# Dense experts of two blocks side by side, and two sparse batches beside two dense ones

## The chip, the cores and the metric

The kernel runs on one core of one Trainium2 chip. The metric is the time of one execution on the device in microseconds, as the median of several runs. The core has five engines that each follow an instruction queue of their own, in order: TensorE (matmuls and transposes; PE in the profile, with PEld for its weight loads), VectorE (DVE), ScalarE (ACT), GpSimd (POOL) and SyncE (SP), which here only starts DMA transfers. An instruction that has to wait for another engine holds up everything behind it in its own queue.

## The reference

The input x has 4 batches of 1024 tokens with 128 numbers each. Four layers follow, each added to x after a layer norm: causal softmax attention (16 heads of 64), an expert layer, linear attention with running sums, and the expert layer again with the same weights. The change concerns the expert layer:

```
logits = einsum('bsh,eh->bse', x, router_w)            # 32 experts
rw = softmax(logits)
vals, idx = top_k(rw, 2)
w_masked = zeros_like(rw) with vals at idx
out = sum over e of (x * w_masked[:, e]) @ W_e          # W_e is 128 x 128
```

Only two weights per token differ from zero, so the same sum can be formed in two ways: with all 32 experts for every token ("dense"), or with two experts for each token after the tokens were sorted by expert ("sparse").

## The kernel before

Tokens are kept in `x_sb` as 32 blocks of 128; a batch is eight blocks, and four blocks are a quarter.

**Dense.** `dense` (L923) takes a list of quarters. For each block it goes through 8 groups `g` of 4 experts: one matmul (recorded as two) into a PSUM tile `pe` of 512 columns (L949), and then the weighting. For the groups in `ACT_GROUPS` (1, 4 and 6) ScalarE scales the four parts into a tile `t` (L957), GpSimd adds the tiles of a block up (L963) and folds the sum in half twice (L977, L978). For the other five groups VectorE does four `scalar_tensor_tensor` each (L966): a part of `pe` times the token's weight, added to `xs`, the block's 128 columns of `x_sb`. All 20 of a block go to the same `xs`, one after the other. `settle` (L931) adds GpSimd's sum two blocks later and stores four finished blocks if wanted. After each group `beside(turn)` is called, so a quarter has 32 turns; also one step of `routed` (L846), which prepares router weights `w` and the transposed tokens of the next quarter.

**Sparse.** `experts` (L197) is a generator for one batch, a chain of steps that end with `yield`. It finds each token's two experts (L209 to L267), counts them with prefix sums on GpSimd and two matmuls (L273 to L290), works out a row for each token and expert (L295 to L333), scales the tokens into tiles `xw` with 8 buffers (L367) and puts closures into `queue` that scatter them to DRAM in 16 indirect DMAs (L357). Each scatter is followed by a small memset (L361). Then comes the pass (L389): 47 tiles of 128 sorted rows in 12 groups of up to four, with 15 iterations. An iteration loads one group of rows (L393), the weights of the group before (L398; for the 15 overflow tiles L402 reads the number of the expert into a register and L405 loads one weight), transposes one group (L424) and multiplies another (L413), which is stored (L419). The flag `passing[0]` lets one chain at a time into the pass. Last, 16 indirect fetches (L432) bring the results back, VectorE adds them (L459, L464), and the batch is stored (L465).

**Order.** The scheduling is manual: each engine's queue has the order in which the Python code emits instructions. After attention there are three stages:

- "f": dense for the two quarters of batch 3, with `fill` (L1094) beside it. It advances two `prepare` generators for linear attention, and takes an entry of `queue` every fourth turn (the fetches of batch 2).
- the linear stage: 32 units, whose first operand is `products(0)` (L1121). In its last units `routed` prepares the first quarter of the next stage.
- "s": dense for six quarters (batches 1 to 3) beside one sparse chain (batch 0). `pieces` (L1237) takes an entry of `queue` every second turn, and calls `on` (L1081) at 5 of 8 turns, or 3 of 8 during the pass. `on` advances each chain by one step if `queue` has at most four entries. What is left after the last turn follows in a plain loop (L1250).

Of the kernel before, what the change touches and what calls it, by code (L numbers as in the profile page):

```python
# [20 lines left out]
def hybrid_kernel(  # L21
# [175 lines left out]
    def experts(b, nm, banks, queue, room, came=None):  # L197
# [80 lines left out]
        yield  # L278

# [102 lines left out]
        while passing[0]:  # L382
            yield
        passing[0] = True
# [4 lines left out]
        for i in range(len(groups) + 3):  # L389
# [19 lines left out]
            if 0 <= i - 3:  # L409
# [9 lines left out]
                nc.sync.dma_start(out=yv[:, g : g + n, :], in_=ys[:, :n, :])  # L419
            if 0 <= i - 2 < len(groups):  # L420
                g, n = groups[i - 2]
                pt = banks[0].tile([P, 512], F32, tag="ps1", name=f"pxs_{nm}_{g}")
                for c in range(n):
                    nc.tensor.transpose(pt[:, c * P : (c + 1) * P], xs[g][:, c, :], ident)  # L424
                xsT[g] = xo.tile([P, 512], F32, tag="xsT", bufs=2, name=f"xsT_{nm}_{g}")
                s_.copy(xsT[g][:, : n * P], pt[:, : n * P])
# [406 lines left out]
    xp = ctx.enter_context(tc.tile_pool(name="xp", bufs=1, reuse_waits="tile"))  # L833
    came = ctx.enter_context(tc.tile_pool(name="came", bufs=3, reuse_waits="tile"))
# [88 lines left out]
    def dense(nm_, qs, store, pool, mp, ps_e, known, beside):  # L923


        due = []
# [12 lines left out]
        for i, q in enumerate(qs):  # L939
# [4 lines left out]
            for c in range(4):  # L944
                xs = x_sb[:, q * 4 + c, :]
                parts = []
                for g in range(E // 4):
                    pe = ps_e.tile([P, 512], F32, tag="e", name=f"pe_{nm_}_{q}_{c}_{g}")
                    nc.tensor.matmul(  # L949
                        pe, xnT[:, c * P : (c + 1) * P],  # L950
                        we_sb[:, 4 * g : 4 * g + 4, :].rearrange("p e d -> p (e d)"),
                        start=True, stop=True,
                    )
                    if g in ACT_GROUPS:
                        t = mp.tile([P, 512], F32, tag="t", name=f"t_{nm_}_{q}_{c}_{g}")
                        for e in range(4):
                            nc.scalar.mul(  # L957
                                t[:, e * D : (e + 1) * D], pe[:, e * D : (e + 1) * D],
                                w[:, c, 4 * g + e : 4 * g + e + 1],
                            )  # L960
                        parts.append(t)
                        if len(parts) > 1:
                            nc.gpsimd.tensor_tensor(parts[0], parts[0], t, ALU.add)  # L963
                    else:
                        for e in range(4):
                            nc.vector.scalar_tensor_tensor(  # L966
                                xs, pe[:, e * D : (e + 1) * D],
                                w[:, c, 4 * g + e : 4 * g + e + 1], xs,
                                ALU.mult, ALU.add,
                            )  # L970
                    if g == 3:
                        settle(2)
                    next(nxt, None)
                    beside(turn)
                    turn += 1
                s = parts[0]
                nc.gpsimd.tensor_tensor(s[:, :256], s[:, :256], s[:, 256:], ALU.add)  # L977
                nc.gpsimd.tensor_tensor(s[:, :D], s[:, :D], s[:, D : 2 * D], ALU.add)  # L978
                due.append((xs, s, q * 4 if c == 3 else None))
# [11 lines left out]
    lb = lin.enter_context(tc.tile_pool(name="lb", bufs=3, reuse_waits="tile"))  # L991
    G = 4
# [87 lines left out]

    def on():  # L1081
# [5 lines left out]
    with ExitStack() as ph:  # L1087
        mp = ph.enter_context(tc.tile_pool(name="mpf", bufs=9, reuse_waits="tile"))
# [5 lines left out]
        def fill(turn):  # L1094

            next(preps[turn % 2], None)
# [17 lines left out]
    with lin as ph:  # L1114
        lp = ph.enter_context(tc.tile_pool(name="lp", bufs=3, reuse_waits="tile"))
# [4 lines left out]

        def products(u):  # L1121

            kq, va = feats[u // G]
            k = kq[:, u % G, :P]
            kv = lp.tile([P, NE, LH, LD], F32, tag="kv", bufs=3, name=f"kv_{u}")
            nc.gpsimd.tensor_tensor(
                kv[:, :LD],
                k.rearrange("p (h d) -> p h d", h=LH).unsqueeze(1).to_broadcast([P, LD, LH, LD]),
                va[:, u % G, :].rearrange("p (h e) -> p e h", e=LD).unsqueeze(3).to_broadcast([P, LD, LH, LD]),
                ALU.mult,  # L1130
            )
            nc.scalar.copy(kv[:, LD].rearrange("p h d -> p (h d)"), k)
            return kv
# [73 lines left out]
        qs = list(range(NB // 4 * 1, NT // 4))  # L1207
        kv = products(0)
# [25 lines left out]
    for b, r in enumerate((room,)):  # L1234
        sides.append(experts(b, f"s{b}", banks, queue, r, came))

    def pieces(turn):  # L1237

        if turn % 2 and queue:
            queue.pop(0)()  # L1240
        if turn % 8 in ((0, 3, 6) if passing[0] else (0, 2, 3, 5, 6)):
            on()

    with ExitStack() as ph:
        mp = ph.enter_context(tc.tile_pool(name="mps", bufs=12, reuse_waits="tile"))
        ps_s = ph.enter_context(tc.tile_pool(name="ps_2", bufs=3, space=PSUM, reuse_waits="tile"))
        ps_e = ph.enter_context(tc.tile_pool(name="ps_es", bufs=5, space=PSUM, reuse_waits="tile"))
# [38 lines left out]
```

## Time and profile before

| | us |
|---|---|
| median of three runs | 2052.43 (2049.49 to 2055.55) |
| the profiled execution | 2047.43 |
| its span, first to last instruction | 2045.7 |
| stage f, first to last dense matmul | 1497.5 to 1579.0 |
| linear stage, first cumulating matmul | 1587.5 |
| stage s, first dense matmul | 1773.5 |
| stage s, loads of the pass | 1897.9 to 1950.4 |
| stage s, fetches | 1960.6 to 1998.4 |
| stage s, last dense matmul ends | 2036.7 |

Over the whole span TensorE is busy 93%, VectorE 75%, ScalarE 60% and GpSimd 56%. Most of it is attention, which the change leaves as it is; so the shares have to be read by stage. The profile gives each group of instructions with its line in the kernel, its engine, the tiles written and read, the number, the busy time and the mean length of one, and the idle time in front of it with what ended it. A timeline row has the start, the length, the engine, the line, the operation and how often it was repeated. Repeated instructions may overlap, so the time from start to start isn't the length of one.

### The profile page before, as it was taken

What the parts mean: (1) busy time and instruction counts of PE and PEld (TensorE: products, weight loads), DVE (VectorE), ACT (ScalarE), POOL (GpSimd) and SP (SyncE); (2) the same over time, 40 slices, a digit from 0 to 9 for tenths busy, and PEclk for the clock granted to TensorE, in tenths of its full rate; (3) what the DMA queues carried; (4) which work ended last, traced back from release to release, by engine and by line L of the source; (5) the groups of instructions that cost most, each with busy time, mean ns of one, the idle gap of its engine ahead of it and who ended that gap; (6) DMA issues with size and microseconds to landing.
All of it is one profiled execution on the core that took longest, in us unless ns stands there. A gap on an engine that the chain in (4) does not pass through costs nothing.

```text
span 2045.7 us, 33584 instructions
## 1 busy us (share of the span) xinstructions
PE 1892.4 (93%) x10066; PEld 1048.2 (51%) x10066; DVE 1539.8 (75%) x4467; ACT 1232.6 (60%) x3889; POOL 1137.9 (56%) x2080
## 2 busy tenths in 40 slices
PE   6999999999999999999999999999877989878886
PEld 3555555555555655555565555556632445433532
DVE  5777776776787767678767677776569788988888
ACT  4766666676676666766666676676464566144433
POOL 3444445444675476456645754674359667348364
PEclk9999999999999999999999999999989999989989
DMA  7000000000003310000141100004211000000510
GB/s 213 1 1 1 1 1 1 1 1 1 1 15 90 96 19 8 1 1 7 57 114 35 15 1 1 1 21 128 60 45 15 1 0 0 1 1 22 164 55 25
DMA packets 111875, 62.54 MB, mean 31 GB/s; under 512 B 5552, under 2 KB 110160, under 8 KB 111568
## 3 DMA queue, kind: packets, MB, share of 16 engines
q1 hardware_dynamic: 101936, 50.43, 8.7%
q0 software_dynamic: 9472, 8.40, 2.1%
q8 instruction: 82, 1.34, 0.3%
q10 hardware_dynamic: 288, 1.57, 0.2%
q14 instruction: 97, 0.79, 0.1%
HBM read 35.60 MB, written 24.77 MB: 30 GB/s over the span
## 4 chain that ended last, share of the span: by engine, by line
PE 61%; DVE 18%; ACT 9%; POOL 7%; issue 4%; DMA 1%; SPq 0%; ACTq 0%; DVEq 0%; POOLq 0%
PE s L581 19%; PE po L687 10%; PE pt L670 10%; DVE nmx L590 6%; DVE x_sb L966 5%; PE pe_s L949 4%; ACT p L615 4%; PE pw L702 3%; PE pk L530 3%; ACT pT L674 2%; PE cum L1152 2%; PE cum L1144 2%; PE pe L413 2%; ACT p L620 1%; PE pv L544 1%
## 5 line engine op out<-in xcount | busy, mean ns | idle before, releaser
L590 DVE TENSOR_REDUCE nmx<-s 128x2 f32<-128x1024 f32 x512 | 604.6, 1220 | 218.5 <-PE s L581 217.9
L615 ACT ACTIVATE p<-s,nmx 128x512 f32<-128x512 f32 (+3 forms) x640 | 360.7, 575 | 312.5 <-DVE nmx L590 281.9
L581 PE MATMUL s<-kT,qT 64*128 64x512 f32 x2048 | 518.0, 619 | 7.8 <-ACT p L615 4.4
L657 POOL TENSOR_SCALAR p<-p,f,ri 128x512 f32<-128x512 f32 (+3 forms) x768 | 502.6, 670 | 0.9 <-issue 0.6
L670 PEld LDWEIGHTS pt<-ident,p 128*128 128x128 f32 x2304 | 249.8, 141 | 219.1 <-issue 91.8
L670 PE MATMUL pt<-ident,p 128*128 128x128 f32 x2304 | 336.0, 282 | 24.4 <-POOL rs L635 7.1
L674 ACT COPY pT<-pt 128x512 f32<-128x512 f32 (+3 forms) x768 | 324.0, 509 | 12.0 <-PE pt L670 9.6
L639 POOL TENSOR_TENSOR rs<-rs,f 128x2 f32<-128x2 f32 x256 | 51.9, 203 | 438.0 <-ACT f L606 408.6
L687 PE MATMUL po<-pT,va 128*64 128x256 f32 (+1 forms) x2560 | 291.1, 365 | 0.6 <-DVE oT L694 0.6
L581 PEld LDWEIGHTS s<-kT,qT 64*128 64x128 f32 x2048 | 173.3, 185 | 195.2 <-issue 94.1
L620 ACT ACTIVATE p<-s,nmx 128x128 f32<-128x128 f32 x512 | 180.3, 365 | 107.5 <-DVE nmx L590 104.8
L687 PEld LDWEIGHTS po<-pT,va 128*64 128x64 f32 x2560 | 167.0, 136 | 97.2 <-issue 32.6
L949 PE MATMUL pe_s<-we_sb,xnT_s 128*128 128x512 f32 x384 | 191.5, 639 | 17.7 <-ACT t_s L957 16.1
L966 DVE SCALAR_TENSOR_TENSOR x_sb<-pe_s,w_s,x_sb 128x128 f32<-128x128 f32 x480 | 166.3, 349 | 26.1 <-PE pe_s L949 10.1
L628 DVE SCALAR_TENSOR_TENSOR p<-p,qtri 128x128 f32<-128x128 f32 x512 | 145.6, 312 | 7.0 <-ACT p L620 3.7
L635 POOL TENSOR_TENSOR rs<-rs 128x2 f32<-128x2 f32 x192 | 43.8, 228 | 187.8 <-DVE ri L648 187.8
L615 ACT ACTIVATION_READ_ACCUMULATOR p<-s,nmx 128x1 f32 x640 | 138.8, 217 | 0.0
L957 ACT ACTIVATE t_s<-pe_s,w_s 128x128 f32<-128x128 f32 x288 | 81.7, 368 | 85.8 <-PE pe_s L949 80.6
L949 PEld LDWEIGHTS pe_s<-we_sb,xnT_s 128*128 128x128 f32 x384 | 72.5, 202 | 115.4 <-issue 46.8
L963 POOL TENSOR_TENSOR t_s<-t_s,t_s 128x512 f32<-128x512 f32 x48 | 61.2, 1275 | 106.8 <-ACT t_s L957 106.5
L707 DVE TENSOR_TENSOR x_sb<-pw,x_sb 128x128 f32<-128x128 f32 x128 | 36.9, 290 | 79.7 <-PE pw L702 79.6
L702 PE MATMUL pw<-wo_sb,oT 128*128 128x128 f32 x512 | 84.4, 289 | 1.8 <-DVE x_sb L707 1.0
(302 smaller groups left out, 2683.0 us busy)
## 6 DMA issues: line engine op xcount, KB each, us to landing
xs<-xs_d SPq DMA_DIRECT2D x33, 256.0 KB, 3.1
ys_d<-ys SPq DMA_DIRECT2D x33, 256.0 KB, 2.4
we<-_ffn_expert_weights_dram SPq DMA_DIRECT2D x24, 256.0 KB, 3.6
xs_d<-zero SPq DMA_DIRECT2D x2, 3008.0 KB, 17.5
we<-_ffn_expert_weights_dram SPq DMA_DIRECT2D x45, 64.0 KB, 1.7
xs_s<-xs_d SPq DMA_DIRECT2D x11, 256.0 KB, 3.2
ys_d<-ys_s SPq DMA_DIRECT2D x11, 256.0 KB, 2.5
we_sb<-_ffn_expert_weights_dram SPq DMA_DIRECT2D x4, 512.0 KB, 6.2
```

The source lines that it names most:

```text
L581: nc.tensor.matmul(st[:, h, :], self.qT[rows, self.ib * P : (self.ib + 1) * P], self.kT[rows, j * 512 : (j + 1) * 512], start=True, stop=True,
L590: nc.vector.tensor_reduce(self.nmx[:, i, :], self.s[i], AX.X, ALU.max, negate=True)
L615: nc.scalar.activation(self.p[h][:, at : at + m * P], self.s[i][:, h, : m * P], AF.Exp, bias=bias, accum_out=self.rs[:, i, h : h + 1],)
L620: nc.scalar.activation(self.p[h][:, at + m * P : at + (m + 1) * P], self.s[i][:, h, m * P : (m + 1) * P], AF.Exp, bias=bias,)
L628: nc.vector.scalar_tensor_tensor(d, d, 1.0, qtri, ALU.mult, ALU.mult, accum_out=self.rs[:, 2, h : h + 1])
L657: nc.gpsimd.tensor_scalar(w, w, self.f[:, i, h : h + 1], self.ri[:, h : h + 1], ALU.mult, ALU.mult,)
L670: nc.tensor.transpose(pt[:, c * P : (c + 1) * P], self.p[h][:, (g + c) * P : (g + c + 1) * P], ident,)
L674: nc.scalar.copy(self.pTs[h][:, g : g + m, self.col : self.col + P], pt[:, : m * P].rearrange("p (c i) -> p c i", c=m),)
L687: nc.tensor.matmul(po[h * DH : (h + 1) * DH, c0:256], va[:, jb, h, :], pTs[h][:, jb, c0:], start=(jb == 0), stop=(jb == n - 1),)
L702: nc.tensor.matmul(pw[:, :P], oTs[i][:, c * P : (c + 1) * P], wo_sb[:, pr, :], start=(i == 0), stop=(i == len(prs) - 1),)
L949: nc.tensor.matmul(pe, xnT[:, c * P : (c + 1) * P], we_sb[:, 4 * g : 4 * g + 4, :].rearrange("p e d -> p (e d)"), start=True, stop=True,)
L966: nc.vector.scalar_tensor_tensor(xs, pe[:, e * D : (e + 1) * D], w[:, c, 4 * g + e : 4 * g + e + 1], xs, ALU.mult, ALU.add,)
```

## The change

1. `dense` takes two blocks at a time. For each group two matmuls go into two `pe` tiles; ScalarE and GpSimd then treat both blocks, and VectorE alternates between them: expert 0 of the first block, expert 0 of the second, expert 1 of the first, and so on. The two turns of a group follow together. `settle(2)` moves to `g == 0`, and the folding of two blocks stands at the end of a pair. This holds for f and for s.
2. Stage s has dense work for four quarters (batches 2 and 3) and two chains (batches 0 and 1), the second with a `Room` of its own. Both use the one `queue`, and `passing[0]` sets one pass behind the other. `on` is called every second turn, and `queue` is emptied at seven of eight turns.
3. A chain in stage s has `slack` 3: three more empty steps behind the prefix sums, ahead of the pass, and in its iteration 2.
4. `products(0)` for the linear stage is emitted at turn 56 of f, once the preparations are run to their end. In front it stood behind stage f.
5. Buffers: tiles `t` 9 to 12 in f and 12 to 18 in s; in s the PSUM banks are 6 for dense and 2 for the rest, from 5 and 3. The pools `xp` and `came` are made when the linear stage's are given back.

```diff
-    def experts(b, nm, banks, queue, room, came=None):
+    def experts(b, nm, banks, queue, room, came=None, slack=0):
...
         yield
+        for _ in range(slack):
+            yield
 
         pc = banks[0].tile([P, 512], F32, tag="ps1", name=f"pc_{nm}")
...
         while passing[0]:
+            yield
+        for _ in range(slack):
             yield
         passing[0] = True
...
+            if i == 2:
+                for _ in range(slack):
+                    yield
             if 0 <= i - 2 < len(groups):
...
-            for c in range(4):
-                xs = x_sb[:, q * 4 + c, :]
-                parts = []
+            for c0 in (0, 2):
+                parts = [[], []]
                 for g in range(E // 4):
...
+                    pes = []
+                    for c in (c0, c0 + 1):
+                        pe = ps_e.tile([P, 512], F32, tag="e", name=f"pe_{nm_}_{q}_{c}_{g}")
+                        nc.tensor.matmul(
+                            pe, xnT[:, c * P : (c + 1) * P],
+                            we_sb[:, 4 * g : 4 * g + 4, :].rearrange("p e d -> p (e d)"),
+                            start=True, stop=True,
+                        )
+                        pes.append(pe)
                     if g in ACT_GROUPS:
...
+                    else:
+
                         for e in range(4):
...
-                            nc.vector.scalar_tensor_tensor(
-                                xs, pe[:, e * D : (e + 1) * D],
-                                w[:, c, 4 * g + e : 4 * g + e + 1], xs,
-                                ALU.mult, ALU.add,
-                            )
-                    if g == 3:
+                            for c, pe in zip((c0, c0 + 1), pes):
+                                xs = x_sb[:, q * 4 + c, :]
+                                nc.vector.scalar_tensor_tensor(
+                                    xs, pe[:, e * D : (e + 1) * D],
+                                    w[:, c, 4 * g + e : 4 * g + e + 1], xs,
+                                    ALU.mult, ALU.add,
+                                )
+                    if g == 0:
                         settle(2)
-                    next(nxt, None)
-                    beside(turn)
-                    turn += 1
...
+                    for _ in range(2):
+                        next(nxt, None)
+                        beside(turn)
+                        turn += 1
...
-        mp = ph.enter_context(tc.tile_pool(name="mpf", bufs=9, reuse_waits="tile"))
+        mp = ph.enter_context(tc.tile_pool(name="mpf", bufs=12, reuse_waits="tile"))
...
+            if turn == 56:
+                for p in preps:
+                    for _ in p:
+                        pass
+                feats["kv"] = products(0)
             next(preps[turn % 2], None)
...
-        qs = list(range(NB // 4 * 1, NT // 4))
-        kv = products(0)
+        qs = list(range(NB // 4 * 2, NT // 4))
+        kv = feats.pop("kv")
...
-    for b, r in enumerate((room,)):
-        sides.append(experts(b, f"s{b}", banks, queue, r, came))
+    xp = ctx.enter_context(tc.tile_pool(name="xp", bufs=1, reuse_waits="tile"))
+    came = ctx.enter_context(tc.tile_pool(name="came", bufs=3, reuse_waits="tile"))
+    for b, r in enumerate((room, Room(xp, "b"))):
+        sides.append(experts(b, f"s{b}", banks, queue, r, came, 3))
 
     def pieces(turn):
 
-        if turn % 2 and queue:
+        if turn % 8 != 7 and queue:
             queue.pop(0)()
-        if turn % 8 in ((0, 3, 6) if passing[0] else (0, 2, 3, 5, 6)):
+        if turn % 2 and sides:
             on()
...
-        mp = ph.enter_context(tc.tile_pool(name="mps", bufs=12, reuse_waits="tile"))
-        ps_s = ph.enter_context(tc.tile_pool(name="ps_2", bufs=3, space=PSUM, reuse_waits="tile"))
-        ps_e = ph.enter_context(tc.tile_pool(name="ps_es", bufs=5, space=PSUM, reuse_waits="tile"))
+        mp = ph.enter_context(tc.tile_pool(name="mps", bufs=18, reuse_waits="tile"))
+        ps_s = ph.enter_context(tc.tile_pool(name="ps_2", bufs=2, space=PSUM, reuse_waits="tile"))
+        ps_e = ph.enter_context(tc.tile_pool(name="ps_es", bufs=6, space=PSUM, reuse_waits="tile"))
```

## The prediction

> **What bounds the kernel now.** I read the table of stretches first, to place the stages: attention until about 1497 us, the first dense stage ("f") 1497 to 1585, linear attention 1585 to 1773, and the second expert layer ("s") from 1773 to the end. The change touches f and s. In both, VectorE is the busiest (75.5 of 85 us, 233.5 of 269):
>
> ```profile
> core 0: us, PE busy (x) PEld busy (x) DVE busy (x) ACT busy (x) POOL busy (x), PEclk, DMA share, GB/s
> 1500.00:1585.00 85.00, 65.94 (x147) 25.41 (x145) 75.49 (x220) 45.92 (x132) 68.61 (x60) 0.95 0.10 12
> 1773.00:2042.00 269.00, 219.19 (x615) 101.57 (x615) 233.53 (x756) 104.55 (x345) 142.34 (x177) 0.92 0.17 50
> ```
>
> Next VectorE's timeline at the end of s, where nothing but dense work is left:
>
> ```profile
> 2019.41 1.32 DVE L931 TENSOR_TENSOR x_sb<-x_sb,t_s 128x128 f32<-128x128 f32 x1
> 2020.65 7.76 DVE L966 SCALAR_TENSOR_TENSOR x_sb<-pe_s,w_s,x_sb 128x128 f32<-128x128 f32 x20
> 2028.33 1.31 DVE L931 TENSOR_TENSOR x_sb<-x_sb,t_s 128x128 f32<-128x128 f32 x1
> ```
>
> One block takes 8.92 us; 20 accumulations take 7.76, that is 0.388 us from start to start though one lasts 0.351: each waits for the result before it. TensorE needs less: six of its records (three groups) take 2.84 us, of which the last lasts 0.59, so (2.84 - 0.59) / 5 = 0.45 a record at that place, and 0.43 where the pass runs (six in 2.74): 0.86 us a group, 6.9 a block.
>
> **The change, part by part.** A "turn" is one group of one block. Stage s goes from 6 quarters (192 turns) and one sparse chain to 4 quarters (128 turns) and two chains.
>
> *Alternating accumulations.* The nearest row of two independent ones is attention's mask:
>
> ```profile
> 701.45 0.28 DVE L628 SCALAR_TENSOR_TENSOR p<-p,qtri 128x128 f32<-128x128 f32 x1
> 701.66 0.08 DVE L628 DVE_READ_ACCUMULATOR p<-p,qtri 128x1 f32 x1
> 701.66 0.29 DVE L628 SCALAR_TENSOR_TENSOR p<-p,qtri 128x128 f32<-128x128 f32 x1
> ```
>
> The second starts 0.21 us after the first, before it has ended. The Trainium skill, "VectorE: DVE Perf Modes", section "The DRAIN you can't avoid", speaks against the change: the next operation waits for the pipe to empty, and copies chained without semaphores took as long as with them (though it adds that an operation that isn't held starts earlier). By that rule the pitch stays 0.388, 2.5 x 0.388 = 0.97 us a turn; by the row it is 2.5 x 0.21 = 0.53. I take the row; the ends are 0.20 and 0.388. VectorE then drops to 0.53 + settling 0.04 to 0.16 + routing 7.6 us a quarter (the rows of lines 853 to 920 summed) / 32 = 0.24, about 0.9 us a turn, level with TensorE's 0.86 + 0.07 of routing.
>
> *Stage f.* VectorE saves 160 x 0.18 = 28 us, but that isn't all gained. GpSimd's timeline is nearly gapless from 1515.6 to 1584 (68 us): two fetches (1.1 each), two adds (1.6 each), folding (1.3 + 0.7) make some 7.5 us a block beside the preparations, and every one of these remains. Its start moves up by perhaps 4 us. The handover: between the last f matmul and the first cumulating one TensorE sits 8.5 us, with the product of block 0 (2.1 us on GpSimd) after everything else; it now stands at turn 56, before the last eight turns' GpSimd work. It brings about 4 us; the next product still stands behind the backlog. Sum -8 us, ends -3 and -16.
>
> *Linear stage.* Routing for quarter 4 instead of 2, same instructions: 0.
>
> *Stage s, dense part.* I count the chain's steps (yields). Before, steps came at 5 of 8 turns (3 of 8 in the pass): 54 steps put the first sorted load at turn 85, and the trace has it at 1897.9, 1.45 us a turn. After, a step comes every second turn, so 128 turns hold 64. Two chains move in step: sort at step 25, three idle, row numbers at 36, then 32 scatters drained at 7 of 8 turns until turn 109. Chain A starts its pass at step 54 (turn 107), idles three, and is at iteration 7 of 15 when the dense turns end. B has only scattered. What it costs:
> - Turns 0 to 49: VectorE 49 x 0.53 + settling 4 + routing 14 + 2 x 6.5 of chain (rows of lines 209 to 267) = 57, start and first waits 4: 61 us.
> - Turns 49 to 73: GpSimd is in front. One chain had 12.3 us here (sort 3.3, prefixes 3.0, places 2.4 + 1.5, weights 2.5), now two, plus 24 x 0.49 dense, and VectorE waits in line twice (positions, row numbers). Before, 11 turns took 24 us with one chain and TensorE waited 9.0 for the sort. Two chains at once: 42 us, where 24 turns of matmuls and both count matmuls need 28.
> - Turns 73 to 103: scatters.
>
> ```profile
> 1870.76 0.98 POOL L357 DMA_INDIRECT xs_d<-xw_s,row_s  x1 [0.15 <-issue]
> 1871.74 0.12 POOL L361 MEMSET between<- 128x1 f32 x1
> 1872.04 0.96 POOL L357 DMA_INDIRECT xs_d<-xw_s,row_s  x1 [0.19 <-issue]
> ```
>
>   A scatter with its memset and issue gap is 1.28 us; at 7 of 8 turns with 0.49 dense (a block's 3.9 us of adds and folds over 8) that is 1.61 us a turn. ScalarE can't run ahead: it has 8 buffers for scaled rows, and dense products stand behind it. 24 scatters must be done by turn 103: 24 x 1.28 + 30 x 0.49 + 1 = 46 us.
> - Turns 103 to 128: GpSimd's rest is hidden; TensorE 25 x 0.86 + six iterations at 1.3 = 29 us.
> Together 178, I take 180 from first to last dense matmul; before it was 2036.7 - 1773.5 = 263. Ends: 160 (lags overlap) and 200.
>
> *Stage s, what comes after.* 48 steps are left with no dense work. The pass is a pipeline through SyncE's queue, which has this for the overflow tiles:
>
> ```profile
> 1933.88 0.38 SPq L419 DMA_DIRECT2D ys_d<-ys_s  x1
> 1934.36 0.46 SPq L393 DMA_DIRECT2D xs_s<-xs_d  x1
> 1935.90 3.76 SPq L405 DMA_DIRECT2D we_s<-_ffn_expert_weights_dram  x4
> 1939.77 0.38 SPq L419 DMA_DIRECT2D ys_d<-ys_s  x1
> ```
>
> It is contiguous: 5.9 us an iteration for four weights chosen by a register, whatever the engines do; 15 of them are 22 us a pass. An ordinary iteration moves 768 KB; the pass before moved 153 GB/s at a DMA share of 0.54, so 280 at most: 2.8 us, and ScalarE's copy between two matmuls gives 2.2. I take 3.0.
> - A's rest: the last settling and store block SyncE for 5 us, then 27.5 of issues and the last tiles: 33 us.
> - B: loads land 3, seven iterations 21, overflow 22, last tiles 3: 48 us (A's fetches lie beside it).
> - B's fetches wait for the last store (2.4). Back to back they are 1.27 us apart:
>
> ```profile
> 1963.14 0.97 POOL L432 DMA_INDIRECT y_s<-ys_d,row_s  x1
> 1964.42 0.95 POOL L432 DMA_INDIRECT y_s<-ys_d,row_s  x1 [0.31 <-issue]
> ```
>
>   16 x 1.27 = 20, landing 2, add 0.7, store of 512 KB 3.2, close 1.7: 30 us.
> Sum 111, I take 110; before, 2045.7 - 2036.7 = 9. The Trainium skill, "TensorE: Matmul & The Clock Gate", Part 1, has the clock halve after an idle window of some 3.4 us. The trace agrees: four transposes after 5.9 us idle take 1.12 us instead of 0.60. Here TensorE is busy 1.3 of 3 to 6 us. At half clock ordinary iterations would take 3.5, +7 us in all; overflow ones are the queue's and unchanged. With the rule 117, by the row without it 110; ends 101 and 122.
>
> The smaller PSUM pool for chains (2 banks for 3) costs nothing in the pass, where two tiles alternate, and up to 2 us elsewhere. The second room's seven memsets stand at the head of s, where GpSimd waits 20 us for products: 0.
>
> **Sum.** s: 180 + 110 = 290 against 263 + 9 = 272: +18. f and handover -8. Net +10. The profiled run was 2047.43 us (span 2045.70, 1.7 around it), so 2057.4; the median of three lies 5.0 above it: **2062 us**, slower by 0.5%. A measurement can tell about 0.3%, 6 us, from no change.
>
> **Rivals.**
> - *Hidden lag, faster.* The place is turns 49 to 103. Eighteen product buffers let dense work run three pairs ahead of GpSimd's adds, and slack keeps waiting chain steps away from each other. If GpSimd's lag is thus absorbed, the part costs its busiest engine alone (GpSimd 16 x 3.9 + 73 for the chains' sorting and scatters + 6 = 141, TensorE about 140) plus the usual tenth: 155. With a tail of 106 that is 261, -11; with -12 in f, -23: 2029. It decides from a dense part under about 164 on. For it: before, VectorE too ran at 87% through all waits. Against it: the 8 row buffers tie ScalarE to the scatters, and the trace shows it waiting for them (2.1 us) even with one chain. Chance 0.25.
> - *No pitch gained.* If the drain holds, VectorE needs 128 x 0.97 + 16 + 24 + 38 of chains = 202 us in s and f gains only the handover: 205 + 110 - 272 - 4 = +39: 2091. Against it is the mask row; for it, that this source is in PSUM. Chance 0.08.
> - *Even.* The two effects cancel within 6 us: 0.10.
> - *The forecast*, tail outweighs: 0.57, its own range 2059 to 2085.
> Slower is 0.57 + 0.08 = 0.65. For 8 in 10 the range reaches into the first rival and to the second, also where all upper ends meet: 2028 to 2098.
>
> **What would show it.** Pitch: 20 accumulations in about 4.2 us, two blocks interleaved. f: GpSimd gapless to its end, stage shorter by under 12 us. s: last dense matmul 170 to 190 us after the first; GpSimd over 90% busy in the scatters; after it VectorE and TensorE mostly idle for about 110 us, with weight loads in fours every 5.9 us, twice. The forecast is wrong if the dense part ends before 164 us, or if passes run at half the issue time I took.

## The result and the profile after

| | before | after |
|---|---|---|
| median of four runs, us | 2052.19 (2049.49 to 2055.55) | 2088.26 (2087.03 to 2088.99) |
| ratio | | 1.0174, 95% interval 1.0157 to 1.0192 |
| the profiled execution: time, span | 2047.43, 2045.7 | 2087.03, 2085.3 |
| f, first dense matmul, to s, first dense matmul | 276.0 | 277.9 |
| s, first dense matmul to end of the last | 263.2 | 188.6 |
| from there to the end of the span | 9.0 | 122.8 |

The change costs 36 us, where 10 were forecast. In the two profiled executions it is 39.6: stage s begins at 1773.9 instead of 1773.5 (+0.4), its dense part is 74.6 shorter, and 113.8 are added behind it. The forecast had -8, -83 and +101 for the same three. Every one of them missed in the same direction, by 8, 9 and 13 us: 30 in all. (The profiled execution of the kernel before lies 4.8 us under its median and that of the changed one 1.2, so the medians show 36 and not 40.)

The table of stretches of the changed kernel (start:end, length, then the busy time and the count of each engine, the granted clock, the share of busy DMA engines, GB/s) shows stage s from its first dense matmul to the end. Line numbers are now those of the changed kernel: L956 is the dense matmul, L978 VectorE's accumulation, L439 the fetch.

```profile
core 0: us, PE busy (x) PEld busy (x) DVE busy (x) ACT busy (x) POOL busy (x), PEclk, DMA share, GB/s
1773.50:1835.00 61.50, 51.23 (x155) 25.14 (x156) 48.03 (x212) 29.63 (x98) 25.91 (x32) 0.94 0.00 1
1835.00:1880.00 45.00, 32.88 (x81) 14.33 (x79) 34.45 (x160) 14.61 (x52) 31.01 (x50) 0.92 0.02 7
1880.00:1930.00 50.00, 31.28 (x68) 13.42 (x68) 36.39 (x130) 19.43 (x61) 41.38 (x63) 0.77 0.09 31
1930.00:1962.00 32.00, 28.13 (x100) 15.29 (x101) 18.33 (x55) 17.51 (x58) 25.76 (x38) 0.89 0.54 158
1962.00:1994.00 32.00, 20.17 (x91) 15.19 (x89) 7.96 (x20) 3.99 (x7) 2.75 (x5) 0.69 0.59 169
1994.00:2055.00 61.00, 36.64 (x141) 30.11 (x141) 10.29 (x16) 6.91 (x12) 15.23 (x16) 0.50 0.60 169
2055.00:2085.00 30.00, 0.00 (x0) 0.00 (x0) 3.04 (x5) 0.00 (x0) 15.10 (x16) 0.50 0.27 77
```

Before, VectorE was busy 87% of the stage. Now it is busy 57 to 78% of the rows in which dense work lasts (the first four). TensorE is at 83% in the first, falls to 63% in the third, where GpSimd has 83%, and reaches 88% in the fourth, where batch 0's pass runs beside dense work. In the last three rows VectorE works 21 us of 123, and the clock of TensorE stands at half in batch 1's pass (1994 to 2055). The two rows of VectorE's timeline that answer to the blocks of 7.76 us:

```profile
1783.02 2.13 DVE L978 SCALAR_TENSOR_TENSOR x_sb<-pe_s,w_s,x_sb 128x128 f32<-128x128 f32 x8
1785.94 2.13 DVE L978 SCALAR_TENSOR_TENSOR x_sb<-pe_s,w_s,x_sb 128x128 f32<-128x128 f32 x8
```

Eight accumulations take 2.13 us and one lasts 0.341 (the mean of the group), so (2.13 - 0.34) / 7 = 0.256 from start to start, where a dependent one needed 0.388.

### The profile page after: what moved, and what is told of

Same layout as the page of the kernel before. It is cut to its first block, busy times and chain, and to the rows that moved or that the text cites. A ratio compares the mean times of both kernels' runs of the same rounds, so it can differ in the third digit from the quotient of the medians.

```text
span 2085.3 us, 33636 instructions
## 1 busy us (share of the span) xinstructions
PE 1874.0 (90%) x10083; PEld 1062.7 (51%) x10083; DVE 1459.5 (70%) x4307; ACT 1219.4 (58%) x3833; POOL 1151.8 (55%) x2129
## 4 chain that ended last, share of the span: by engine, by line
PE 59%; DVE 15%; ACT 10%; POOL 9%; issue 4%; DMA 1%; SPq 1%; another core or an unknown queue 0%; ACTq 0%; POOLq 0%; DVEq 0%
PE s L588 18%; PE po L694 10%; PE pt L677 10%; DVE nmx L597 6%; ACT p L622 3%; PE pw L709 3%; PE pk L537 3%; ACT pT L681 2%; PE pe_s L956 2%; DVE x_sb L978 2%; PE pe L417 2%; PE pv L551 1%; ACT p L627 1%; PE cum L1162 1%; PE cum L1170 1%
## 5 line engine op out<-in xcount | busy, mean ns | idle before, releaser
L956 PE MATMUL pe_s<-we_sb,xnT_s 128*128 128x512 f32 x256 | 125.7, 640 | 17.0 <-ACT t_s L966 15.6
L978 DVE SCALAR_TENSOR_TENSOR x_sb<-pe_s,w_s,x_sb 128x128 f32<-128x128 f32 x320 | 86.7, 341 | 35.9 <-PE pe_s L956 34.0
L956 PEld LDWEIGHTS pe_s<-we_sb,xnT_s 128*128 128x128 f32 x256 | 50.3, 207 | 79.7 <-issue 44.0
L709 PEld LDWEIGHTS pw<-wo_sb,oT 128*128 128x128 f32 x512 | 68.6, 190 | 29.3 <-ACT pT L681 13.2
L439 POOL DMA_INDIRECT x_sb<-ys_d,row x48 | 76.7, 1599 | 11.1 <-issue 10.7
```

Source lines behind the costliest of these rows:

```text
L709: nc.tensor.matmul(pw[:, :P], oTs[i][:, c * P : (c + 1) * P], wo_sb[:, pr, :], start=(i == 0), stop=(i == len(prs) - 1),)
L956: nc.tensor.matmul(pe, xnT[:, c * P : (c + 1) * P], we_sb[:, 4 * g : 4 * g + 4, :].rearrange("p e d -> p (e d)"), start=True, stop=True,)
L978: nc.vector.scalar_tensor_tensor(xs, pe[:, e * D : (e + 1) * D], w[:, c, 4 * g + e : 4 * g + e + 1], xs, ALU.mult, ALU.add,)
```

## The experiments

Times are medians of four runs (five for the fourth group of experts); the ratio is to the kernel before, run on the same chip. Times from first to last dense matmul and so on come from the profile of the run.

**What each half is worth.** The first kernel has the alternation, but one chain and six dense quarters as before:

```diff
-        qs = list(range(NB // 4 * 2, NT // 4))
+        qs = list(range(NB // 4 * 1, NT // 4))
...
-    for b, r in enumerate((room, Room(xp, "b"))):
-        sides.append(experts(b, f"s{b}", banks, queue, r, came, 3))
+    for b, r in enumerate((room,)):
+        sides.append(experts(b, f"s{b}", banks, queue, r, came))
...
-        if turn % 8 != 7 and queue:
+        if turn % 2 and queue:
...
-        if turn % 2 and sides:
+        if turn % 8 in ((0, 3, 6) if passing[0] else (0, 2, 3, 5, 6)):
```

> Side-by-side dense work alone: stage s keeps six quarters and one chain with the old step rates and no slack, the early first product stays. Theory (the two chains and their tail are what costs, alternation gains): the 16 accumulations of two blocks' group keep a pitch of 0.26 us as in the changed kernel, VectorE drops to about 1.05 us a turn, level with TensorE, stage s takes 235 to 255 us instead of 272, the whole 2015 to 2035 us. Rival (alternation frees an engine that doesn't matter, the loss is in the dense order itself): 2048 us or more.

Measured: 2027.31 us, ratio 0.9882 (0.9861 to 0.9904). The dense part takes 242 us instead of 263. Its table of stretches:

```profile
1773.00:2016.00 243.00, 208.10 (x616) 100.23 (x616) 193.63 (x747) 101.59 (x345) 139.22 (x172) 0.94 0.19 55
```

VectorE has gone from 234 of 269 us to 194 of 243, below TensorE's 208. This half is a gain of 24 us, and the kernel is faster than both others.

The second kernel has two chains, with the dense body from before (one block at a time, all of its 20 accumulations one after the other):

```diff
-            for c0 in (0, 2):
-                parts = [[], []]
+            for c in range(4):
+                xs = x_sb[:, q * 4 + c, :]
+                parts = []
```

> Two chains and four quarters alone, each block by itself as before; buffers, step rates and slack as in the changed kernel. Theory (alternation gains what the two chains then overspend): the dense part of s grows from 189 us to 200 to 225, the tail stays at 120 to 126, the whole 2100 to 2130 us. Rival (dense part set by GpSimd's scatters and the chains' waits alone, alternation is worth nothing there): within 8 us of the changed kernel's 2088.

Measured: 2098.36 us, ratio 1.0230 (1.0207 to 1.0252); dense part 195.5, 123.0 behind it. The whole lies between the two bands, 1.6 us under the theory's and 2.4 above the rival's, and the dense part is under the theory's 200. Two chains cost 46 us by themselves, and beside them the alternation is worth 2098.4 - 2088.3 = 10 us, not 24. In the profiles 7 of the 10 are in the dense part of s, but kernels with the same code there differ by up to 5 us (188.6 to 193.4), so 2 to 7 is all that can be said. VectorE's pitch counts for little in the dense part once two chains stand beside it.

**Stage f: where the gain went.** The changed kernel without batch 2's fetches in f:

```diff
         yield
+        if came is None and b == 2:
+            return
         if came is None:
```

> The changed kernel without the 16 fetches of batch 2 in stage f (the output lacks that batch's first expert layer). In the changed kernel the first dense matmul of f to the first of s took 277.9 us, before 276.0, though the dense matmuls of f ended 8.7 us earlier. Theory (GpSimd's backlog of fetches and adds holds VectorE's settling and the second product, so f's gain cannot come out): without the fetches, about 18 to 25 us of GpSimd work, that stretch falls to 262 to 270 us and the whole to 2073 to 2080. Rival (the gain is lost later in the linear stage, whose other engines set its pace): 274 us or more, the whole within 4 us of 2088.

Measured: 2071.71 us, ratio 1.0089 (1.0072 to 1.0105). From f's first dense matmul to that of s it is 261.5 us, 16.4 less than after and just under the theory's band (the whole is 1.3 under it). So the fetches in GpSimd's queue decide how long the stage takes. The timelines of GpSimd, TensorE and VectorE at the end of f in the changed kernel show how (L991 ends a fold, L1100 makes products, L1162 and L1170 are the cumulating matmuls of a unit):

```profile
1574.81 2.64 POOL L1100 TENSOR_TENSOR kv<-kq,va 128x1024 f32<-128x1024 f32 x1
...
1583.74 0.45 POOL L991 TENSOR_TENSOR t_f<-t_f 128x128 f32<-128x128 f32 x1
1584.15 2.12 POOL L1100 TENSOR_TENSOR kv<-kq,va 128x1024 f32<-128x1024 f32 x1
```

```profile
1577.50 4.21 PE L1162 MATMUL cum<-kv,mtri 128*128 128x384 f32 x6 [7.23 <-POOL kv L1100]
1587.73 4.21 PE L1170 MATMUL cum<-kv,rest 128*128 128x384 f32 x6 [6.02 <-DVE m L1182]
1591.72 2.25 PE L1162 MATMUL cum<-kv,mtri 128*128 128x384 f32 x6
```

```profile
1583.01 0.80 DVE L937 TENSOR_TENSOR x_sb<-x_sb,t_f 128x128 f32<-128x128 f32 x1 [5.21 <-POOL t_f L991]
```

And in the kernel before:

```profile
1583.65 0.45 POOL L978 TENSOR_TENSOR t_f<-t_f 128x128 f32<-128x128 f32 x1
```

```profile
1587.48 3.61 PE L1144 MATMUL cum<-kv,mtri 128*128 128x384 f32 x6 [8.51 <-POOL kv L1126]
...
1592.86 2.10 PE L1144 MATMUL cum<-kv,mtri 128*128 128x384 f32 x6
```

The dense matmuls now end at 1570.3 instead of 1579.0, 8.7 us earlier. GpSimd ends its dense work at 1584.2, as before (1584.1). The first product does come early, and TensorE starts at 1577.5. But VectorE must settle the last two blocks before it takes up the first unit's result, and they wait for GpSimd's folds until 1583.0; so TensorE waits again (6.02). The second unit's matmuls start at 1591.7, where they started at 1592.9 before. To see what the early product alone does, the product was put back behind f:

```diff
-                feats["kv"] = products(0)
...
-        kv = feats.pop("kv")
+        kv = products(0)
```

> The changed kernel with products(0) back in its place after stage f (the preparations end as they did before). Theory (GpSimd's backlog, not the place of the first product, sets when the linear stage runs): the first cumulating matmul comes about 4 us later, but the first dense matmul of s moves by less than 3 us, and the whole stays within 6 us of the changed kernel's 2088. Rival (the early product is worth its forecast 4 us and something else in f loses 8): the whole is 4 to 8 us longer.

Measured: 2081.91 us, ratio 1.0137 (1.0120 to 1.0154). Its TensorE timeline:

```profile
1583.59 4.21 PE L1161 MATMUL cum<-kv,mtri 128*128 128x384 f32 x6 [13.98 <-POOL kv L1100]
...
1589.71 2.10 PE L1161 MATMUL cum<-kv,mtri 128*128 128x384 f32 x6
```

The first unit is 6.1 us later, the second 2.0 earlier (1589.7), and s begins at 278.4 us after f's first matmul, against 277.9. Seven kernels that have the early product and two chains, with the same f, show 275.5 to 278.6 there, so the early product gains nothing that can be told from their spread. The rival falls. The whole is 0.1 us under the theory's band, but not by the product: batch 1's pass took 54.5 us here and 61.1 in the changed kernel, of which more below.

**The dense part of s.** In the forecast, turn 49 came 61 us after the first dense matmul. In the trace its matmuls stand at 67.6, and the sort behind them at 71. (They stand at 67.6 to 71.0 in the eight kernels that have this code.) So the chains were held back by 25 steps, which leaves dense work alone in these turns:

```diff
+        if came is not None:
+            for _ in range(25):
+                yield
         room.busy = True
```

> The changed kernel with 25 empty steps at the head of both chains in s, so that they begin at turn 50 and the first 49 turns have dense work alone. Theory (the 71 us of turns 0 to 49, forecast as 61, come from two chains' steps between dense work whose engines then wait for each other; dense alone runs at TensorE's 0.86 to 0.95 us a turn): the dense matmuls of turn 49 stand 44 to 50 us after the first of s instead of about 67, and the end after the last dense matmul grows by 20 to 35 us. Rival (dense alone takes most of the 71 us, by routing and by ScalarE's late tiles): turn 49 stands at 58 us or later.

Measured: 2105.80 us, ratio 1.0263 (1.0244 to 1.0281). TensorE's timeline, two records to a turn:

```profile
1776.11 11.63 PE L959 MATMUL pe_s<-we_sb,xnT_s 128*128 128x512 f32 x24
...
1790.21 3.61 PE L959 MATMUL pe_s<-we_sb,xnT_s 128*128 128x512 f32 x8
...
1794.47 22.56 PE L959 MATMUL pe_s<-we_sb,xnT_s 128*128 128x512 f32 x52
...
1817.41 2.16 PE L959 MATMUL pe_s<-we_sb,xnT_s 128*128 128x512 f32 x4 [0.38 <-ACT t_s L969]
...
1821.05 3.60 PE L959 MATMUL pe_s<-we_sb,xnT_s 128*128 128x512 f32 x8
...
1825.29 8.83 PE L959 MATMUL pe_s<-we_sb,xnT_s 128*128 128x512 f32 x20
```

96 records lie ahead of the last row, and turn 49 (the 99th record) stands 50.1 us after the first, at the edge of the theory's band: 48 were forecast for dense work alone (61 less 13 for the chains). In the changed kernel the row that holds it (with 96 records ahead of it too) stands later:

```profile
1840.56 5.49 PE L956 MATMUL pe_s<-we_sb,xnT_s 128*128 128x512 f32 x12
```

The chains' first 25 steps add 17 us here (17 to 21 in the eight kernels), not 13. They move VectorE's own rows in between, and TensorE then waits for normalized tokens (L873 and ScalarE's L231: 2.68, 0.72, 2.11, 1.48 and 0.89 us). With the chains held back the dense part is 29 us shorter, but the end grew by 47, more than the 20 to 35 expected: steps left behind the dense part are dearer there than beside it.

In the middle of s TensorE's timeline of the changed kernel has the large gaps:

```profile
1883.39 0.48 PE L884 MATMUL pxn_s<-ident,xn_s 128*128 128x128 f32 x1 [13.18 <-DVE xn_s L873]
...
1889.56 0.73 PE L884 MATMUL pxn_s<-ident,xn_s 128*128 128x128 f32 x2 [5.00 <-DVE xn_s L873]
...
1913.65 13.56 PE L956 MATMUL pe_s<-we_sb,xnT_s 128*128 128x512 f32 x24 [7.32 <-ACT t_s L966]
1933.83 2.08 PE L956 MATMUL pe_s<-we_sb,xnT_s 128*128 128x512 f32 x2 [6.62 <-ACT t_s L966]
```

In front of the first, VectorE stands at the positions, which GpSimd makes for both chains:

```profile
1875.54 0.42 DVE L325 TENSOR_REDUCE pos_s<-u_s 128x8 f32<-128x256 f32 x1 [9.62 <-POOL u_s L322]
```

It then works off its positions and 16 late accumulations before the tokens (L873). In front of the second it works without a break through row numbers and weights of both chains (L335 to L341). The last two are ScalarE's: between 1880 and 1935 its scaled rows (L369) wait 21.2 us for scatters to give back one of eight buffers, and the dense products stand behind them. With more buffers:

```diff
-                    t = xo.tile([P, D], F32, tag="xw", bufs=8, name=f"xw_{nm}_{cc_}_{j}")
+                    t = xo.tile([P, D], F32, tag="xw", bufs=15, name=f"xw_{nm}_{cc_}_{j}")
```

> The changed kernel with 15 buffers for scaled rows instead of 8. ScalarE waited 22.9 us for scatters, and TensorE stood 7.3 and 6.6 us behind it. Theory (the buffers tie ScalarE's dense products to GpSimd's scatters): the two waits of TensorE shrink below 3 us together, dense part of s from 189 to 175 to 182 us, the whole 6 to 13 us shorter. Rival (GpSimd is full there, with products and scatters in one queue, and the dense work waits for it in any case): less than 4 us.

Measured: 2080.48 us, ratio 1.0132 (1.0115 to 1.0149); the dense part is 181.1. In its TensorE timeline the two gaps are gone, while the 13.20 and 4.99 in front of L884 remain:

```profile
1919.66 5.59 PE L956 MATMUL pe_s<-we_sb,xnT_s 128*128 128x512 f32 x12 [1.10 <-issue]
1927.17 8.40 PE L956 MATMUL pe_s<-we_sb,xnT_s 128*128 128x512 f32 x15 [1.91 <-issue]
```

The tie of ScalarE to the scatters was worth 8 us. (Kernels that leave the dense part as it is show 188.6 to 193.4 for it, so the 188.6 is at the low end, and the dense part gains 8 to 12.)

**Batch 1's pass.** It took 61.1 us from its first load (1994.57) to the end of its last store. SyncE's timeline of the changed kernel (L423 stores), where the fetches of batch 0 are over:

```profile
2026.50 0.36 SPq L423 DMA_DIRECT2D ys_d<-ys_s  x1
...
2030.16 0.36 SPq L423 DMA_DIRECT2D ys_d<-ys_s  x1
...
2036.04 0.38 SPq L423 DMA_DIRECT2D ys_d<-ys_s  x1
```

From store to store an ordinary iteration takes 3.66 us, an overflow one 5.88. The 3.66 is 0.66 more than forecast, and of the iterations before, beside the fetches, one takes 10.69. VectorE's timeline:

```profile
2005.07 0.69 DVE L466 TENSOR_TENSOR x_sb<-x_sb,y_s 128x512 f32<-128x512 f32 x1 [11.24 <-DMA y_s<-ys_d,row_s]
2005.68 0.69 DVE L422 COPY ys_s<-pe_s 128x512 f32<-128x512 f32 x1
2008.55 0.69 DVE L422 COPY ys_s<-pe_s 128x512 f32<-128x512 f32 x1 [2.19 <-issue]
2019.24 0.69 DVE L422 COPY ys_s<-pe_s 128x512 f32<-128x512 f32 x1 [10.00 <-remote]
```

An addition of batch 0's fetched rows waits 11.24 us at the head of the queue, and the copy that the pass needs stands behind it: it starts 3.0 us after the recorded end of its matmuls. A later copy waits 10.00, with nothing ahead of it in VectorE's queue. Three kernels take the causes away one at a time and together. First, without the fetches and additions of batch 0:

```diff
         yield
+        if came is not None and b == 0:
+            nc.sync.dma_start(out=out_v[b], in_=x_sb[:, c0 : c0 + NB, :])
+            return
```

> The changed kernel without the 16 fetches and four additions of batch 0 (its output lacks the second expert layer; the batch is still stored). In the changed kernel they lie beside the second pass, whose ordinary iterations were slow until the last fetch had landed. Theory (VectorE's additions wait for fetches with the second pass's copies queued behind them, and fetches compete with its loads): first load to last store of the second pass falls from 61 us to 50 to 54, the whole to 2078 to 2082. Rival (the slow TensorE clock alone stretches that pass): the pass stays at 58 us or more, the whole at 2085 or more.

Measured: 2078.65 us, ratio 1.0126 (1.0095 to 1.0157); the pass takes 53.0 us, and all ordinary iterations are now 3.66. The fetches cost the pass 8 us. Two other kernels split these 8: the one with the late product and the one with the late chains have the same end, fetches and additions included, and passes of 54.5 and 54.2 us. VectorE's timeline in the former, the addition and the copy that answers to the one of 10.00:

```profile
2008.58 0.69 DVE L466 TENSOR_TENSOR x_sb<-x_sb,y_s 128x512 f32<-128x512 f32 x1 [10.89 <-DMA y_s<-ys_d,row_s]
...
2015.72 0.69 DVE L422 COPY ys_s<-pe_s 128x512 f32<-128x512 f32 x1 [2.97 <-PE pe_s L417]
```

The addition holds the first copy by 3.0 us there too, but no later copy is late. So the addition at the head of VectorE's queue costs the pass 1.2 to 1.5 us (a part is caught up in the next iteration), and the long wait behind it the other 6.6. Of eight kernels with batch 0's fetches beside this pass, six have long waits (passes of 59.3 to 61.3 us) and these two have none. Second, TensorE kept busy by an unused matmul after each step behind the dense part:

```diff
             on()
+            hot = ps_e.tile([P, 512], F32, tag="e", name=f"hot_{k}")
+            nc.tensor.matmul(
+                hot, ident, we_sb[:, 0:4, :].rearrange("p e d -> p (e d)"), start=True, stop=True
+            )
+            k += 1
```

> The changed kernel with one unused matmul of 512 columns behind each step after the last dense turn, to keep TensorE's clock up. Theory (clock stretches ordinary iterations from about 2.8 to 3.66 us): granted clock in the second pass rises from 0.50 to over 0.8, its last ordinary iterations fall below 3.1 us, the whole is 3 to 6 us shorter. Rival (fetches and queue set the pass): iterations stay at 3.5 us or more though the clock is up, the whole changes by less than 2 us.

Measured: 2089.09 us, ratio 1.0177 (1.0153 to 1.0201). The clock is 0.84 over the pass instead of 0.50, and ordinary iterations clear of the fetches take 2.33 us. But the whole is the same: the pass takes 61.1 us, as before, because the waits beside the fetches grew by about what was saved. Each theory had half of it. Third, both edits together:

> The changed kernel with both earlier edits of its end: one unused 512-column matmul after each step behind the dense part, and batch 0's 16 fetches and 4 additions left out (it is stored unfinished). Theory (the pass of batch 1 has two separate causes of its 60.7 us, half clock and the fetches beside it): every ordinary iteration takes about 2.3 to 2.6 us, the pass is 3 + 7 x 2.4 + 22 + 3 = 43 to 47 us, and the whole lands near 2088 - 15 = 2070 to 2076. Rival (the pass is held by SyncE's queue and the loads, not by the clock): iterations shorten, but the pass stays near the 52.7 us of the run without fetches alone, and the whole at 2077 to 2082.

Measured: 2076.88 us, ratio 1.0115 (1.0098 to 1.0132). Rows of its SyncE timeline, then of TensorE's, where eight matmuls and four transposes of an iteration take about half of what they took at half clock (2.07 and 1.06 us):

```profile
2009.52 0.36 SPq L423 DMA_DIRECT2D ys_d<-ys_s  x1
...
2011.84 0.36 SPq L423 DMA_DIRECT2D ys_d<-ys_s  x1
```

```profile
2009.93 1.16 PE L417 MATMUL pe_s<-we_s,xsT_s 128*128 128x128 f32 x8
2010.92 0.60 PE L431 MATMUL pxs_s<-ident,xs_s 128*128 128x128 f32 x4
```

Three iterations take 2.33 us and two more 3.09 and 2.71; the pass takes 47.9, and it is 108.9 us from the last dense matmul to the end. The fetches (8 us) and the clock (5 us) are separate and together make the 13 us. The pass is 0.9 us above the theory's band and the whole 0.9 too, with a dense part of 193.2, the long end of the spread named above. The whole falls just short of the rival's band; the pass, 4.8 us under the rival's 52.7, decides.

That the clock does this and not the unused matmuls is seen in two runs that have none. One row of TensorE's timeline from the run without batch 0's fetches (granted clock 0.50 from 2006 to 2032), and one from the run without f's fetches, where the clock rose by itself (0.88 from 2012 to 2018, then 1.00 until 2024):

```profile
2011.43 2.08 PE L417 MATMUL pe_s<-we_s,xsT_s 128*128 128x128 f32 x8 [0.73 <-ACT xsT_s L433]
```

```profile
2015.87 1.16 PE L417 MATMUL pe_s<-we_s,xsT_s 128*128 128x128 f32 x8 [0.73 <-ACT xsT_s L433]
```

The next burst follows after 3.66 us in the first, after 2.33 in the second.

Why the copy at 2019.24 waited so long was asked with a memset behind each fetch in s, as each scatter has:

```diff
+            if came is not None:
+                g_.memset(between, 0.0)
```

> The changed kernel with a one-column memset on GpSimd behind each fetch of stage s, as each scatter has one. While the fetches of batch 0 ran back to back, copies of the second pass started 3 to 11 us after the recorded end of the matmuls they wait for. Theory (the row of indirect transfers on GpSimd, issued without a break, delays others): the memset breaks it, first load to last store of the second pass falls from 61 to 53 to 56 us, the whole by 4 us or more. Rival (the stalls come from the data's way or from the additions that wait in VectorE's queue): pass 59 us or more, the whole within 3 us of 2088.

Measured: 2090.26 us, ratio 1.0181 (1.0164 to 1.0198); the pass is 59.3 us and the long waits remain (one iteration takes 12.41). The theory falls, and the cause stays open.

**A better version.** Two variants of the kernel with the alternation and one chain. With a fourth group of experts on ScalarE and GpSimd in s:

```diff
-                    if g in ACT_GROUPS:
+                    if g in (ACT_GROUPS if nm_ == "f" else (1, 3, 5, 7)):
```

> Side-by-side dense work, one chain and six quarters (2027 us), and in stage s four of eight groups on ScalarE and GpSimd instead of three. VectorE was busy 197 of 247 us there, TensorE 208, GpSimd 143. Theory (VectorE and its waits still set the pace between the chain's steps): VectorE falls by 192 x 0.125 x 4 x 0.26 = 25 us, stage s by 5 to 12 us, the whole 2015 to 2022. Rival (TensorE and the chain's waits for GpSimd set it, and GpSimd gets 31 us more): no gain, 2025 or more.

Measured: 2044.90 us, ratio 0.9959 (0.9945 to 0.9974), 17.6 us longer than with three groups; the dense part is 260 instead of 242. The rival was right that there is no gain. Why so much is lost isn't shown: the places of the groups have changed too, and the 18 product buffers now last for two pairs of blocks instead of three. And with the 15 buffers for scaled rows:

> One sparse batch and six dense quarters with the alternating body, as in the first experiment (2027.3), but with 15 buffers for scaled rows instead of 8. Theory (with one chain the eight buffers tie ScalarE to half as many scatters as with two): 2 to 5 us shorter than 2027, since two chains gave 8. Rival (with one chain ScalarE is never late by more than the dense work's own slack): the same, 2025 to 2029.

Measured: 2026.80 us, ratio 0.9872 (0.9856 to 0.9888): no different from 2027.31. With one chain the eight buffers don't hold up the dense work. The alternation with one chain is the best kernel of the study.

## Why the prediction was right in its direction and wrong in its size

That the tail outweighs what the dense part saves was right. What failed are the sizes of three terms, which together are the 30 us: f's gain (-8 forecast, none measured), the dense part of s (180 forecast, 188.6 measured) and batch 1's pass (48 forecast, 61.1 measured). In the table A is batch 0's chain and B batch 1's.

| term of the sum | forecast | measured | what showed it |
|---|---|---|---|
| f and the handover | -8 | 0 (start of s +0.4) | fetches left out: -16; late product: the same |
| s to turn 49 | 61 | 67.6 (sort at 71) | late chains: 50.1 for dense work alone |
| turns 49 to 73 | 42 | 44.6, sort to first scatter | |
| scatters and rest of the dense part | 75 | 73 | 15 buffers: 8 of it gone |
| A's rest | 33 | 32.1 | |
| B's pass | 48 | 61.1 | no fetches: 53.0; and TensorE's clock up: 47.9 |
| B's fetches, the end | 30 | 29.6 | |

- **Pitch.** The row was the better guide: 0.256, nearer to the 0.21 of the mask than to the 0.388 that the drain would keep. The rival "no pitch gained" forecast 2091, near the measured time, but what it rests on didn't happen: that it came near is luck.
- **Stage f.** This step failed. The prediction saw GpSimd "nearly gapless" and still let its work move up by "perhaps 4 us", and gave the early product 4 more. GpSimd's end didn't move, and the wait for the product was replaced at once by VectorE's settling behind the same backlog, in the queue ahead of the unit's result. A saving on VectorE and TensorE was counted where a third engine was full.
- **Dense part of s.** The terms for GpSimd's stages were close. Dense work alone was right within about 2 us. The step that failed is the chains' first 25 steps: they were charged with VectorE's busy time (13 us) and cost 17 to 21, since each of them also makes TensorE wait, and the sort comes at 71 instead of 61. The tie of ScalarE to eight buffers, which the prediction named, was a real cost of 8 us, within its terms. (GpSimd's five terms for one chain add up to 12.7, not 12.3; nothing hangs on it.) The point of 164 us, below which the change would have been faster, was missed by 25.
- **B's pass.** This is the largest miss: 13 of 30 us. Two steps failed. "A's fetches lie beside it" was costed at nothing, and they cost 8: up to 1.5 because an addition stands in VectorE's queue ahead of the copies of the pass, and 6.6 by the long wait, which came with the fetches in six of eight kernels and whose cause stays open. And the prediction chose 3.0 us for an ordinary iteration without the clock rule, where it had 3.5 with it. The half clock that the rule (the Trainium skill, "TensorE: Matmul & The Clock Gate", Part 1) gave did come: the granted clock is 0.50 in that stretch, four transposes take 1.06 us and eight matmuls 2.05, and the iteration takes 3.66 where it takes 2.33 at full clock. It was worth 53.0 - 47.9 = 5 us. But idle windows of some 3.4 us don't explain why it stayed: in the later iterations of the run without fetches TensorE's gaps are 0.73 us and the clock is still 0.50. With both causes removed the pass is 47.9 and the end 108.9, where 48 and 110 were forecast. That this is so close is in part luck: the pass's own terms add up to 49, and the iterations were then mostly faster than the 3.0 of the sum.
- **What wasn't separated.** The 18 us in front of the transposes at 1883 and 1889 (positions, row numbers and weights of two chains at once) were not tested by themselves, nor were the three empty steps and the split of the PSUM banks with two chains. The three misses (8, 9, 13) were all on the same side, so 2088 lies above the forecast's own range (2059 to 2085) and near the end of the wide one, which was made for errors that partly cancel.

Taken together: the alternation gains 24 us alone. Two chains take 64 turns of dense work away, but add 114 us behind the dense part, in which VectorE and TensorE have little to do; they cost 46 alone, and they take away most of what the alternation could give: the large gaps of TensorE in the dense part are then waits for GpSimd's positions, for the chains' rows on VectorE and for ScalarE behind the scatters.

## What to carry to other kernels

Work that is taken off a full engine gains only until the next queue that is already gapless, and it is there that the gain has to be read: here GpSimd's end in f did not move, whatever VectorE and TensorE saved. A serial chain costs what is left of it when the parallel work beside it runs out, so count its steps against the turns that remain before adding a second chain. And where a transfer "lies beside" a pipeline, don't put it at nothing: its consumer can stand in an in-order queue ahead of the pipeline's own instructions (1.5 us here), and what else it costs has to be measured (6.6 here, by a wait that nobody foresaw). In such a tail TensorE's clock need not be that of the dense stage: here it was 0.50 against 0.94.

## What the runs showed of the hardware

- Independent accumulations from PSUM on VectorE start 0.256 us apart while each lasts 0.341; dependent ones 0.388 (0.351 each).
- In this pass, with gaps of about 0.7 us in front of each burst of eight matmuls, both clocks occur: 0.50 in the run without batch 0's fetches (2006 to 2032), 1.00 in the run without f's fetches (2018 to 2024). What decides between them isn't shown. An unused 512-column matmul behind each step brought 0.84 over the pass.
- Beside the fetches, consumers of TensorE's results started late. These are rows of TensorE and ScalarE in the changed kernel; VectorE's copy of the first row's result is the one at 2019.24 above.

```profile
2012.93 2.07 PE L417 MATMUL pe_s<-we_s,xsT_s 128*128 128x128 f32 x8 [3.56 <-ACT xsT_s L433]
2014.79 1.06 PE L431 MATMUL pxs_s<-ident,xs_s 128*128 128x128 f32 x4
```

```profile
2019.36 0.58 ACT L433 COPY xsT_s<-pxs_s 128x512 f32<-128x512 f32 x1 [6.49 <-remote]
```

The matmuls are recorded until 2015.00 and the transposes until 2015.85, but VectorE's copy of the one starts 4.2 us after and ScalarE's of the other 3.5 us after, within 0.12 us of each other. GpSimd was issuing fetches 1.25 us apart until 2016.6. A memset behind each fetch changed nothing. With the fetches left out it doesn't occur, but the fetches alone don't make it: with the late product or the late chains they are issued at the same 1.25 us and no copy behind the first is late. The profile models the ends of TensorE's rows, so a late signal can't be told from TensorE itself ending late. The cause is open.
